# Query and output projections by seven half products each, in a decoder layer on one core

## The chip, the core and the metric

The kernel runs on one core of a Trainium2 chip. The core has an engine for matrix products (PE, whose loads of stationary weights are listed apart as PEld), three engines for other arithmetic (DVE, ACT, POOL) and a queue, SP, that issues all of this kernel's DMAs. [...] PE writes its products into banks of PSUM, DVE and ACT move them from there into SBUF, and POOL works from SBUF to SBUF. The metric is the device time of one execution in microseconds.

## What is computed

The input `x` is four sequences of 2048 positions with 512 features (float32). One pre-norm decoder layer is applied:

```python
x = x + attn(layernorm(x))                # a linear recurrence along the axis of length 4
x = x + xattn(layernorm(x), ctx)          # 16 heads of 32, 77 keys a sequence
x = x + ffn(layernorm(x))                 # 512 -> 2048, butterflies, gelu, butterflies, 2048 -> 512

def xattn(query, context, Wq, Wk, Wv, Wo):
    Q = (query @ Wq.T).reshape(B, T_q, 16, 32)
    K, V = ...                            # from the context, 77 rows
    attn = softmax(Q @ K / sqrt(32))
    return (attn @ V).reshape(B, T_q, 512) @ Wo.T
```

The change concerns `Q` and the product with `Wo`.

## The kernel before

The 2048 positions are cut into 16 blocks `u` of 128. A block holds all four steps `t` of the first axis, so that its `x` is a tile `xt` of 128 positions by 4 steps by 512 features.

Everything that comes ahead of the feed-forward part of a block is the generator `front` (L430). In order: `normed_pairs`, the recurrence as products with fixed taps (`ps_s`, L440), a second norm, the query projection (`ps_q`, L452), the attention steps, the output projection, and a third norm. A norm (`normed`, L402) takes statistics of the four steps on DVE (L377 to L390), then for each step scales on DVE (`xn`, L396), transposes on PE (`ps_t`, L399) and copies on ACT into `xnt` (L400), which holds features on partitions.

- The query projection makes four groups of 128 outputs. Each adds up four products of 512 columns (four steps of 128 positions) in one bank, and ACT copies it to `qt` (L454).
- For each step `t`, four score products go to `ps_sc` (L463), DVE takes maximum and difference (L467, L468), ACT the exponential (L469), DVE sum and reciprocal (L471, L472), and POOL scales the probabilities `pr` (L473). One step later PE transposes them in four groups (`ps_pt`, L483), DVE and ACT copy each group into one of four `pt` tiles, `ps_o` (L494) multiplies them with the values, and DVE copies that to `ot` (L497). Then, for this step alone, four products of 512 columns with `wo` go to `ps_w` (L501), and DVE adds the bank to `xt` (L502).

All banks of `front` carry the tag `f`, of which there are two.

The feed-forward part (`feed_forward`, L522) multiplies by the scheme of Winograd and Strassen: a product of 2x2 halves made by seven products of halves and some sums. The weights are combined before the loop and kept in DRAM (`up7`, `dn7`); `combine` (L510) makes the sums of the block's input, and DVE, ACT and POOL those of the results. All its products have 256 columns (L546, L611). Its weights come by DMA into three rotating buffers (`wts`).

While block `u` is in `feed_forward`, `front` of block `u+1` is woven in: after each pair of products `step` (L531) counts, and at every third count it calls `front` on to its next `yield`. There are 112 counts and 32 yields. A scheduler then sets the order of each engine's instructions. Block 0 has nothing to be woven into but the preparation of the weights (`_prepare`, L213), which runs once at the start; block 15's feed-forward part runs alone at the end.

`wq` and `wo` lie in SBUF through the whole program (L361, L362) and are loaded once (L666, L667).

Of the kernel before, what the change touches and what calls it, by code (L numbers as in the profile page):

```python
# [23 lines left out]
NB = HID // P  # L24
# [188 lines left out]
def _prepare(nc, pool, banks, dram, ident, wexp_t, up_low, up_high, up_bias, dn_low, dn_high, wcon, wup, wdn, bias,  # L213
# [10 lines left out]
    t = wdn  # L224
# [17 lines left out]
    ub = pool.tile([P, NB], F32, name="ub")  # L242
# [4 lines left out]
    nc.sync.dma_start(out=ub, in_=up_bias)  # L247
# [5 lines left out]
    e = _low_products(nc, low, False)  # L253
# [3 lines left out]
    for b in range(NB):  # L257
        ps = banks()
# [33 lines left out]
    nc.vector.tensor_tensor(bias, b1, ub, ALU.add)  # L292
# [16 lines left out]
    src = wcon.rearrange("(p m) d -> p m d", m=NB)  # L309
# [3 lines left out]
    for m in range(NB):  # L313
        ps = banks()
# [5 lines left out]
    src = rows_dn.rearrange("(b p) d -> p b d", p=P)  # L320
# [3 lines left out]
    for b in range(NB):  # L324
        ps = banks()
# [5 lines left out]
    b11, b12, b21, b22 = (wdn[:, r * h : r * h + h, c * (D // 2) : (c + 1) * (D // 2)] for r in range(2) for c in range(2))  # L331
    t1, t2, t3, n4 = (wup[:, i, :].rearrange("p (b d) -> p b d", b=h) for i in range(4))
# [14 lines left out]
def kernel(ctx: ExitStack, tc: tile.TileContext, x, ctx_t, ssm_vec, ssm_vt, ssm_vinv, wq_t, wk_t, wv_t,  # L347
                        wo_t, wexp_t, up_low, up_high, up_bias, dn_low, dn_high, wcon, b_con, down_bias, out):
    nc = tc.nc
    const = ctx.enter_context(tc.tile_pool(name="const", bufs=1))  # L350
    xpool = ctx.enter_context(tc.tile_pool(name="x", bufs=1))
    work = ctx.enter_context(tc.tile_pool(name="work", bufs=2))
    small = ctx.enter_context(tc.tile_pool(name="small", bufs=2))
    dram = ctx.enter_context(tc.tile_pool(name="dram", bufs=1, space=bass.MemoryType.DRAM))
    psum = ctx.enter_context(tc.tile_pool(name="psum", bufs=2, space=bass.MemoryType.PSUM))
# [5 lines left out]
    wq = const.tile([P, NC, D], F32, name="wq")  # L361
    wo = const.tile([P, NC, D], F32, name="wo")  # L362
    hbias = const.tile([P, NB], F32, name="hbias")
    ybias = const.tile([P, D], F32, name="ybias")
    make_identity(nc, ident)
# [61 lines left out]
                yield  # L427
        res.append(xpt)

    def front(u, xt, res):  # L430


        got = []
        yield from normed_pairs(xt, got)
        xpt = got.pop()
        for c in range(NC):
            ps = psum.tile([P, T, P], F32, tag="f", name="ps_s")
            for f in range(P // NS):
                for i in range(T // 2):
                    nc.tensor.matmul(ps[:, 2 * i : T, f * NS : (f + 1) * NS], lhsT=xpt[:, i, c * (P // NS) + f, :],  # L440
                                     rhs=gt[:, 0 : T - 2 * i, :], start=i == 0, stop=i == T // 2 - 1)
            xc = xt[:, :, c * P : (c + 1) * P]
            nc.vector.tensor_tensor(xc, ps, xc, ALU.add)
            yield

        yield from normed(xt, got)
        xnt = got.pop()
        qt = work.tile([P, NC, T, P], F32, tag="qt", bufs=1, name="qt")
        for g in range(NC):
            ps = psum.tile([P, T, P], F32, tag="f", name="ps_q")  # L450
            for c in range(NC):
                nc.tensor.matmul(ps, lhsT=wq[:, c, g * P : (g + 1) * P], rhs=xnt[:, c, :, :],  # L452
                                 start=c == 0, stop=c == NC - 1)
            nc.scalar.copy(qt[:, g, :, :], ps)  # L454
            yield

        probs = [None] * T
        for t in range(T + 1):
            if t < T:
                pr = work.tile([P, NH, NK], F32, tag="pr", name="pr")  # L460
                for g in range(NC):
                    ps = psum.tile([P, 512], F32, tag="f", name="ps_sc")
                    nc.tensor.matmul(ps[:, 0 : 4 * NK], lhsT=qt[:, g, t, :], rhs=kbd[:, t, g, :], start=True, stop=True)  # L463
                    sc = ps[:, 0 : 4 * NK].rearrange("p (j k) -> p j k", j=4)
                    mx = small.tile([P, 4], F32, tag="mx", bufs=4, name="mx")
                    pg = pr[:, 4 * g : 4 * g + 4, :]
                    nc.vector.tensor_reduce(mx, sc, AX.X, ALU.max)  # L467
                    nc.vector.tensor_tensor(pg, sc, mx.unsqueeze(2).to_broadcast([P, 4, NK]), ALU.subtract)  # L468
                    nc.scalar.activation(pg, pg, AF.Exp, scale=1.0 / math.sqrt(DH))  # L469
                sm = small.tile([P, NH], F32, tag="sm", name="sm")  # L470
                nc.vector.tensor_reduce(sm, pr, AX.X, ALU.add)  # L471
                nc.vector.reciprocal(sm, sm)  # L472
                nc.gpsimd.tensor_tensor(pr, pr, sm.unsqueeze(2).to_broadcast([P, NH, NK]), ALU.mult)  # L473
# [5 lines left out]
            pts = []  # L479
            for g in range(NC):  # L480
                pt_ps = psum.tile([P, 4, P], F32, tag="f", name="ps_pt")
                for j in range(4):
                    nc.tensor.transpose(pt_ps[0:NK, j, :], pr[:, 4 * g + j, :], ident)  # L483
                pt = work.tile([NK, 4, P], F32, tag="pt", bufs=4, name="pt")
                if g % 2:
                    nc.scalar.copy(pt, pt_ps[0:NK])
                else:
                    nc.vector.tensor_copy(pt, pt_ps[0:NK])
                pts.append(pt)
            po = psum.tile([P, NC, P], F32, tag="f", name="ps_o")  # L490
            for g in range(NC):
                for j in range(4):
                    h = 4 * g + j
                    nc.tensor.matmul(po[j * DH : (j + 1) * DH, g, :], lhsT=vsb[:, tt, h * DH : (h + 1) * DH],  # L494
                                     rhs=pts[g][:, j, :], start=True, stop=True, tile_position=(0, j * DH))
            ot = work.tile([P, NC, P], F32, tag="ot", bufs=1, name="ot")
            nc.vector.tensor_copy(ot, po)  # L497
            yield
            ps = psum.tile([P, D], F32, tag="f", name="ps_w")
            for g in range(NC):  # L500
                nc.tensor.matmul(ps, lhsT=ot[:, g, :], rhs=wo[:, g, :], start=g == 0, stop=g == NC - 1)  # L501
            nc.vector.tensor_tensor(xt[:, tt, :], ps, xt[:, tt, :], ALU.add)  # L502
            yield
# [18 lines left out]
    def feed_forward(u, xt, rhs, other):  # L522
# [7 lines left out]

        def step():  # L531
            slot[0] += 1
            if slot[0] % 3 == 0:
                next(other, None)

        def bank(tag):
# [115 lines left out]
        return psum.tile([P, 512], F32, tag="abc"[turn[0]], name="ps_p")  # L652

    up7 = [dram.tile([P, 7, 2, P], F32, name=f"up7_{p}") for p in range(NB // 2)]
    dn7 = [dram.tile([P, NB // 2, D // 2], F32, name=f"dn7_{i}") for i in range(7)]
    xts = {0: load_x(0)}
    ready = []
    with tc.tile_pool(name="prep", bufs=1) as pool:
        wup = pool.tile([P, NC, HID], F32, name="wup")
        wdn = pool.tile([P, NB, D], F32, name="wdn")  # L660
        _recurrence_taps(nc, pool, psum, ssm_vec, ssm_vt, ssm_vinv, gt)
        prep = _prepare(nc, pool, banks, dram, ident, wexp_t, up_low, up_high, up_bias, dn_low, dn_high, wcon,
                        wup, wdn, hbias, up7, dn7)
        next(prep)
        _keys_values(nc, psum, ctx_t, wk_t, wv_t, kbd, vsb, wup)
        nc.sync.dma_start(out=wq, in_=wq_t.rearrange("(c p) e -> p c e", p=P))  # L666
        nc.sync.dma_start(out=wo, in_=wo_t.rearrange("(c p) e -> p c e", p=P))  # L667
# [5 lines left out]
        first = front(0, xts.pop(0), ready)  # L673
        for _ in prep:
            next(first, None)
        for _ in first:
            pass
# [80 lines left out]
```

## Time and profile before

| What | Value |
|---|---|
| Median of 3 runs | 2728.86 us (2724.36 to 2729.57) |
| Profiled execution | 2727.85 us, span 2726.1 us |
| First product of a feed-forward part | starts at 237.95 us |
| Period of one block in the loop | 159.0 us |
| PE records of ps_q, of ps_w (128x512) | 512, 512 |
| PE records of L546 and L611 (128x256) | 3584, 3584 |
| DMA | 320.84 MB, mean 118 GB/s |

The profile is one execution taken by the hardware profiler, in microseconds unless ns is written. A line names a source line (L452), an engine, and the tile written. An fp32 product is two MATMUL records. Busy times of PE include the modelled end of its pipeline, so records overlap; starts are better than lengths for a rate. What stands in brackets behind a group, as in `[0.90 <-DVE xn L396]`, is how long the engine was idle ahead of it and what ended that. The chain of waits starts at the last instruction and goes back each time to what released it.

The DMA queue's rows for weights, with engine, count, size of one and median time to landing:

```profile
w_up<-up SPq DMA_DIRECT2D x128, 896.0 KB, 4.6
w_dn<-dn SPq DMA_DIRECT2D x112, 1024.0 KB, 4.8
```

### The profile page before, as it was taken

The page shows a single profiled execution, that of the slowest core. Times are in us where ns is not written, and L with a number is a line of the kernel's source. Part 1 is how long each engine was busy: PE and PEld are TensorE (multiplying, and loading weights), DVE is VectorE, ACT ScalarE, POOL GpSimd, SP SyncE. Part 2 cuts the span into 40 slices and gives each one's busy share as a digit, 9 for nine tenths or more (in the row PEclk, how much of TensorE's full clock was granted, in tenths as well). Part 3 has the DMA queues.
Part 4 walks back from the last instruction along what each step waited for, and adds up shares of the span by engine and source line. Part 5 has one row for each costly group of instructions (what it writes and reads, how often), then busy time and mean ns, then how long its engine had stood idle before and what let it go on. Part 6 is the DMA issues. An engine that isn't in the chain of part 4 may idle for free.

```text
span 2726.1 us, 34675 instructions
## 1 busy us (share of the span) xinstructions
PE 2626.3 (96%) x13448; PEld 2013.5 (74%) x13448; DVE 1308.1 (48%) x3148; ACT 794.3 (29%) x1456; POOL 778.7 (29%) x918
## 2 busy tenths in 40 slices
PE   6887999999999999999999999999999999999999
PEld 4545777786877778687777868777786877778688
DVE  4375544545454454545445454544545454454531
ACT  0222414223241422324142232414223241422321
POOL 4233231413223141322314132231413223141323
PEclk9888999999999999999999999999999999999999
DMA  7664233242423324242332424233232423323244
GB/s 234 213 246 173 89 111 110 78 135 78 143 89 112 111 76 135 78 143 89 113 109 77 135 78 143 89 114 109 76 136 78 143 89 111 112 77 120 78 141 137
DMA packets 96724, 320.84 MB, mean 118 GB/s; under 512 B 17584, under 2 KB 44336, under 8 KB 80432
## 3 DMA queue, kind: packets, MB, share of 16 engines
q1 hardware_dynamic: 96560, 318.62, 34.5%
q8 instruction: 107, 1.75, 0.2%
q14 instruction: 57, 0.47, 0.0%
HBM read 278.47 MB, written 40.12 MB: 117 GB/s over the span
## 4 chain that ended last, share of the span: by engine, by line
PE 83%; DVE 10%; POOL 4%; DMA 1%; issue 1%; ACT 0%; SPq 0%; POOLq 0%; DVEq 0%; ACTq 0%
PE ps_a L611 10%; PE ps_b L546 10%; PE ps_w L501 8%; PE ps_q L452 8%; PE ps_b L611 7%; PE ps_c L546 7%; PE ps_a L546 6%; PE ps_c L611 5%; PE ps_sc L463 5%; PE ps_pt L483 4%; PE ps_s L440 3%; POOL pr L473 2%; PE ps_t L399 2%; PE ps_o L494 2%; DVE st L377 2%
## 5 line engine op out<-in xcount | busy, mean ns | idle before, releaser
L589 POOL TENSOR_TENSOR s<-a,a 128x256 f32<-128x256 f32 x128 | 92.9, 726 | 1120.1 <-ACT a L551 1120.1
L546 PE MATMUL ps_b<-tb,w_up 128*128 128x256 f32 x1536 | 397.0, 379 | 0.7 <-DVE tb L518 0.7
L611 PE MATMUL ps_a<-w_dn,a 128*128 128x256 f32 x1536 | 372.1, 381 | 0.0
L611 PEld LDWEIGHTS ps_a<-w_dn,a 128*128 128x128 f32 x1536 | 282.3, 190 | 57.4 <-issue 20.3
L546 PEld LDWEIGHTS ps_b<-tb,w_up 128*128 128x128 f32 x1536 | 285.9, 190 | 51.1 <-issue 14.5
L551 ACT ACTIVATE a<-a,hbias 128x256 f32<-128x256 f32 x384 | 192.3, 508 | 270.4 <-DVE a L584 206.9
L546 PE MATMUL ps_a<-xnt,w_up 128*128 128x256 f32 x1024 | 269.0, 380 | 0.0
L611 PE MATMUL ps_c<-w_dn,s 128*128 128x256 f32 x1024 | 235.4, 381 | 7.3 <-POOL s L589 7.3
L501 PE MATMUL ps_w<-wo,ot 128*128 128x512 f32 x512 | 236.2, 604 | 4.8 <-DVE ot L497 4.8
L452 PE MATMUL ps_q<-xnt,wq 128*128 128x512 f32 x512 | 231.9, 596 | 0.7 <-ACT xnt L400 0.7
L611 PEld LDWEIGHTS ps_c<-w_dn,s 128*128 128x128 f32 x1024 | 191.0, 190 | 36.8 <-POOL s L589 11.4
L546 PEld LDWEIGHTS ps_a<-xnt,w_up 128*128 128x128 f32 x1024 | 190.4, 191 | 31.2 <-issue 7.2
L473 POOL TENSOR_TENSOR pr<-pr,sm 128x1232 f32<-128x1232 f32 x64 | 146.1, 2282 | 173.1 <-DVE sm L472 162.9
L501 PEld LDWEIGHTS ps_w<-wo,ot 128*128 128x128 f32 x512 | 96.3, 193 | 107.1 <-issue 94.4
L452 PEld LDWEIGHTS ps_q<-xnt,wq 128*128 128x128 f32 x512 | 97.9, 192 | 98.1 <-issue 93.9
L400 ACT COPY xnt<-ps_t 128x512 f32<-128x512 f32 x128 | 72.2, 588 | 331.4 <-PE ps_t L399 331.2
L469 ACT ACTIVATE pr<-pr 128x308 f32<-128x308 f32 x256 | 107.0, 455 | 206.7 <-DVE pr L468 206.2
L463 PE MATMUL ps_sc<-kbd,qt 128*128 128x308 f32 x512 | 163.3, 430 | 3.3 <-DVE pr L468 3.0
L483 PE MATMUL ps_pt<-ident,pr 128*77 128x128 f32 x1024 | 145.4, 281 | 19.2 <-POOL pr L473 13.6
L483 PEld LDWEIGHTS ps_pt<-ident,pr 128*77 128x77 f32 x1024 | 119.3, 150 | 56.5 <-POOL pr L473 19.7
L502 DVE TENSOR_TENSOR xt<-ps_w,xt 128x512 f32<-128x512 f32 x64 | 44.3, 692 | 235.0 <-PE ps_w L501 235.0
L599 POOL TENSOR_TENSOR xt<-xt,ybias 128x256 f32<-128x256 f32 x128 | 100.2, 818 | 184.4 <-DVE xn L396 184.4
(173 smaller groups left out, 3936.4 us busy)
## 6 DMA issues: line engine op xcount, KB each, us to landing
w_up<-up SPq DMA_DIRECT2D x128, 896.0 KB, 4.6
w_dn<-dn SPq DMA_DIRECT2D x112, 1024.0 KB, 4.8
xt<-in_x SPq DMA_DIRECT2D x16, 1024.0 KB, 5.5
out<-xt SPq DMA_DIRECT2D x64, 256.0 KB, 4.9
wdn<-in_wexp_t SPq DMA_DIRECT2D x4, 1024.0 KB, 10.9
rows_up<-wdn SPq DMA_DIRECT2D x16, 256.0 KB, 2.1
wdn<-rows_up SPq DMA_DIRECT2D x4, 1024.0 KB, 9.0
wdn<-in_wcon SPq DMA_DIRECT2D x4, 1024.0 KB, 4.8
```

The lines of the kernel that those rows point to most:

```text
L440: nc.tensor.matmul(ps[:, 2 * i : T, f * NS : (f + 1) * NS], lhsT=xpt[:, i, c * (P // NS) + f, :], rhs=gt[:, 0 : T - 2 * i, :], start=i == ...
L452: nc.tensor.matmul(ps, lhsT=wq[:, c, g * P : (g + 1) * P], rhs=xnt[:, c, :, :], start=c == 0, stop=c == NC - 1)
L463: nc.tensor.matmul(ps[:, 0 : 4 * NK], lhsT=qt[:, g, t, :], rhs=kbd[:, t, g, :], start=True, stop=True)
L469: nc.scalar.activation(pg, pg, AF.Exp, scale=1.0 / math.sqrt(DH))
L473: nc.gpsimd.tensor_tensor(pr, pr, sm.unsqueeze(2).to_broadcast([P, NH, NK]), ALU.mult)
L483: nc.tensor.transpose(pt_ps[0:NK, j, :], pr[:, 4 * g + j, :], ident)
L501: nc.tensor.matmul(ps, lhsT=ot[:, g, :], rhs=wo[:, g, :], start=g == 0, stop=g == NC - 1)
L546: nc.tensor.matmul(ps, lhsT=w[:, c, :], rhs=rhs[i - 1][:, c], start=first and c == 0, stop=c == 1, skip_group_check=True)
L551: nc.scalar.activation(out, x, AF.Gelu, bias=hbias[:, b : b + 1])
L589: nc.gpsimd.tensor_tensor(s1, a21, a22, ALU.add)
L599: nc.gpsimd.tensor_tensor(r, r, ybias[:, d], ALU.add)
L611: nc.tensor.matmul(ps[:, t, :], lhsT=act[p][lhs[i]][:, t, :], rhs=w[:, p, :], start=first and p == 0 and t == 0, stop=p == h - 1, skip_gro ...
```

## The change

Both projections are made by seven products of halves. Weights, input and output are each cut in 2x2 halves. A new generator runs the seven:

```diff
+    def seven(order, lhs, rhs, two, made):
+        tiles = {}
+        for i in order:
+            key = {2: 1, 7: 6, 4: 6, 3: 5}.get(i, i)
+            if key == i:
+                tiles[i] = psum.tile([P, 2, 2 * P], F32, tag="f", name=f"ps_{two}")
+            for r in range(2):
+                for k in range(2):
+                    nc.tensor.matmul(tiles[key][:, r, :], lhsT=lhs(i, r, k), rhs=rhs(i, r, k),
+                                     start=key == i and r == 0 and k == 0, stop=k == 1, skip_group_check=True)
+            made[i](tiles[key])
+            yield
```

Each of the seven is four matmuls of 256 columns, and `made[i]` is its eviction. Products 2, 7, 4 and 3 go on in the bank of an earlier one, after that one has been read. The order is 1, 6, 2, 7, 5, 4, 3.

For the query projection two sums and a difference of the input are made on POOL and DVE, in place where possible, and the results are put together in `qt`:

```diff
-        for g in range(NC):
-            ps = psum.tile([P, T, P], F32, tag="f", name="ps_q")
-            for c in range(NC):
-                nc.tensor.matmul(ps, lhsT=wq[:, c, g * P : (g + 1) * P], rhs=xnt[:, c, :, :],
-                                 start=c == 0, stop=c == NC - 1)
-            nc.scalar.copy(qt[:, g, :, :], ps)
-            yield
+        if wq is None:
+            wq = work.tile([P, 7, NC // 2, D // 2], F32, tag="pt", bufs=1, name="wq")
+            nc.sync.dma_start(out=wq, in_=wq7)
+        nc.gpsimd.tensor_tensor(t3, b22, b12, ALU.subtract)
+        nc.vector.tensor_tensor(b12, b12, b11, ALU.subtract)
+        nc.vector.tensor_tensor(t2, b22, b12, ALU.subtract)
+        right = {1: b11, 2: b21, 3: b22, 4: b21, 5: b12, 6: t2, 7: t3}
+        def second(ps):
+            moved(q11)(ps)
+            nc.gpsimd.tensor_tensor(b21, b21, t2, ALU.subtract)
+        yield from seven((1, 6, 2, 7, 5, 4, 3), ...,
+                         {1: moved(q21), 6: plus(q12, q21), 2: second, 7: plus(q22, q21), 5: plus(q22, q22),
+                          4: plus(q21, q21), 3: plus(q12, q12)})
```

`moved` is an ACT copy of a bank, `plus` a DVE add of a bank and a tile. The seven weights of the query projection no longer stay in SBUF: they are made once (four sums on POOL), stored to DRAM (`wq7`, 1792 KB), and loaded again for each block from 1 on, into the one buffer that the block's `pt` tile takes afterwards. Those of the output projection (`wo`, seven halves) stay in SBUF.

The attention steps keep their work but for the output projection, and `ot` now holds all four steps; `pt` is one tile of four groups with one buffer instead of four tiles. After the last step the output projection runs for all four at once:

```diff
+        nc.gpsimd.tensor_tensor(s1, a21, a22, ALU.add)
+        nc.vector.tensor_tensor(s2, s1, a11, ALU.subtract)
+        nc.gpsimd.tensor_tensor(s3, a11, a21, ALU.subtract)
+        nc.gpsimd.tensor_tensor(s4, a12, s2, ALU.subtract)
+        left = {1: a11, 2: a12, 3: s4, 4: a22, 5: s1, 6: s2, 7: s3}
+        def onto(r):
+            return lambda ps: nc.vector.tensor_tensor(r, ps, r, ALU.add)
+        def spread(ps):
+            nc.scalar.copy(w1, ps)
+            for r in (r12, r22, r21):
+                nc.gpsimd.tensor_tensor(r, r, w1, ALU.add)
+        yield from seven((1, 6, 2, 7, 5, 4, 3), ...,
+                         {1: spread, 6: onto(r12), 2: onto(r11), 7: onto(r22), 5: onto(r22), 4: onto(r21), 3: onto(r12)})
```

`front` has 38 yields now, and `step` spreads them evenly over the first 104 of the 112 counts (`slot[0] * 38 // 104`). The load of `up_bias` goes straight to `hbias`, whose tile saves the small one `ub`.

More of the change, by code (lines that the diff above doesn't have):

```diff
@@ L246, in _prepare @@
     nc.sync.dma_start(out=high, in_=up_high)
-    nc.sync.dma_start(out=ub, in_=up_bias)
+    nc.sync.dma_start(out=bias, in_=up_bias)
     src = wexp_t.rearrange("(b p) d -> p b d", p=P)
@@ L291, in _prepare @@
     nc.sync.dma_start(out=b1, in_=brow[1, :].rearrange("(b p) -> p b", p=P))
-    nc.vector.tensor_tensor(bias, b1, ub, ALU.add)
+    nc.vector.tensor_tensor(bias, b1, bias, ALU.add)
     h, k = HID // 2, NC // 2
@@ L448, in front, with plus, moved @@
         qt = work.tile([P, NC, T, P], F32, tag="qt", bufs=1, name="qt")
-        for g in range(NC):
-            ps = psum.tile([P, T, P], F32, tag="f", name="ps_q")
-            for c in range(NC):
-                nc.tensor.matmul(ps, lhsT=wq[:, c, g * P : (g + 1) * P], rhs=xnt[:, c, :, :],
-                                 start=c == 0, stop=c == NC - 1)
-            nc.scalar.copy(qt[:, g, :, :], ps)
-            yield
+        if wq is None:
+            wq = work.tile([P, 7, NC // 2, D // 2], F32, tag="pt", bufs=1, name="wq")
+            nc.sync.dma_start(out=wq, in_=wq7)
+        b11, b12, b21, b22 = (xnt[:, c : c + 2, t : t + 2, :] for c in (0, 2) for t in (0, 2))
+        q11, q12, q21, q22 = (qt[:, c : c + 2, t : t + 2, :] for c in (0, 2) for t in (0, 2))
+        t3, t2 = (work.tile([P, 2, 2, P], F32, tag="xn", name="tq") for _ in range(2))
+        nc.gpsimd.tensor_tensor(t3, b22, b12, ALU.subtract)
+        nc.vector.tensor_tensor(b12, b12, b11, ALU.subtract)
+        nc.vector.tensor_tensor(t2, b22, b12, ALU.subtract)
+        right = {1: b11, 2: b21, 3: b22, 4: b21, 5: b12, 6: t2, 7: t3}
+        def plus(out, x):
+            return lambda ps: nc.vector.tensor_tensor(out, ps.rearrange("p r (t q) -> p r t q", t=2), x, ALU.add)
+        def moved(out):
+            return lambda ps: nc.scalar.copy(out, ps.rearrange("p r (t q) -> p r t q", t=2))
+        def second(ps):
+            moved(q11)(ps)
+            nc.gpsimd.tensor_tensor(b21, b21, t2, ALU.subtract)
+        yield from seven((1, 6, 2, 7, 5, 4, 3), lambda i, r, k: wq[:, i - 1, k, r * P : (r + 1) * P],
+                         lambda i, r, k: right[i][:, k, :, :], "q",
+                         {1: moved(q21), 6: plus(q12, q21), 2: second, 7: plus(q22, q21), 5: plus(q22, q22),
+                          4: plus(q21, q21), 3: plus(q12, q12)})
         probs = [None] * T
+        ot = work.tile([P, NC, T, P], F32, tag="xnt", bufs=2, name="ot")
         for t in range(T + 1):
@@ L478, in front @@
             pr, tt = probs[t - 1], t - 1
-            pts = []
+            pts = work.tile([P, NC, 4, P], F32, tag="pt", bufs=1, name="pt")
             for g in range(NC):
@@ L494, in front @@
                     nc.tensor.matmul(po[j * DH : (j + 1) * DH, g, :], lhsT=vsb[:, tt, h * DH : (h + 1) * DH],
-                                     rhs=pts[g][:, j, :], start=True, stop=True, tile_position=(0, j * DH))
-            ot = work.tile([P, NC, P], F32, tag="ot", bufs=1, name="ot")
-            nc.vector.tensor_copy(ot, po)
+                                     rhs=pts[0:NK, g, j, :], start=True, stop=True, tile_position=(0, j * DH))
+            nc.vector.tensor_copy(ot[:, :, tt, :], po)
             yield
[L499 to L503, printed above, removed]
+        a11, a12, a21, a22 = (ot[:, g : g + 2, t : t + 2, :] for t in (0, 2) for g in (0, 2))
+        r11, r12, r21, r22 = (xt[:, t : t + 2, d : d + D // 2] for t in (0, 2) for d in (0, D // 2))
+        sw = work.tile([P, 4, 2, 2, P], F32, tag="qt", bufs=1, name="sw")
+        s1, s2, s3, s4 = (sw[:, i] for i in range(4))
+        nc.gpsimd.tensor_tensor(s1, a21, a22, ALU.add)
[3 more added lines that the diff above has]
+        left = {1: a11, 2: a12, 3: s4, 4: a22, 5: s1, 6: s2, 7: s3}
+        w1 = work.tile([P, 2, 2 * P], F32, tag="xn", name="w1")
+        def onto(r):
[4 more added lines that the diff above has]
+                nc.gpsimd.tensor_tensor(r, r, w1, ALU.add)
+        yield from seven((1, 6, 2, 7, 5, 4, 3), lambda i, r, k: left[i][:, k, r, :], lambda i, r, k: wo[:, i - 1, k, :], "w",
+                         {1: spread, 6: onto(r12), 2: onto(r11), 7: onto(r22), 5: onto(r22), 4: onto(r21), 3: onto(r12)})
         yield from normed(xt, got)
@@ L532, in step @@
             slot[0] += 1
-            if slot[0] % 3 == 0:
+            for _ in range(slot[0] * 38 // 104 - (slot[0] - 1) * 38 // 104):
                 next(other, None)
@@ L672 @@
         xts[1] = load_x(1)
-        first = front(0, xts.pop(0), ready)
+        first = front(0, xts.pop(0), ready, wq)
         for _ in prep:
```

28 lines of the change are left out of this document (20 added, 8 removed).

## The prediction

> **What bounds the kernel now.** I read the page's busy shares first, then the busy times of three equal stretches, then the timeline of PE, and last the chain of waits for the rate of each product.
>
> ```profile
> span 2726.1 us, 34675 instructions
> PE 2626.3 (96%) x13448; PEld 2013.5 (74%) x13448; DVE 1308.1 (48%) x3148; ACT 794.3 (29%) x1456; POOL 778.7 (29%) x918
> ...
> 859.00:1018.00 159.00, 156.41 (x818) 121.33 (x817) 77.47 (x188) 48.47 (x89) 44.39 (x50) 1.00 0.32 106
> 1018.00:1177.00 159.00, 156.42 (x818) 121.33 (x817) 77.48 (x188) 48.47 (x89) 44.39 (x50) 1.00 0.31 106
> ```
>
> The columns of the stretches are length, then PE, PEld, DVE, ACT and POOL busy, the granted clock, the DMA share and GB/s. The loop over blocks repeats every 159.0 us, PE is busy for 156.4 of them at clock 1.00, and every other engine has half its time free. So a block is worth what PE issues plus 2.6 us of waits, and the timeline of PE names these:
>
> ```profile
> 913.53 1.08 PE L399 MATMUL ps_t<-ident,xn 128*128 128x128 f32 x8 [0.90 <-DVE xn L396]
> ...
> 956.73 1.10 PE L483 MATMUL ps_pt<-ident,pr 128*77 128x128 f32 x8 [0.91 <-POOL pr L473]
> ...
> 963.51 1.13 PE L611 MATMUL ps_c<-w_dn,s 128*128 128x256 f32 x4 [0.49 <-POOL s L589]
> ...
> 1014.78 1.06 PE L399 MATMUL ps_t<-ident,xn 128*128 128x128 f32 x8 [0.29 <-DVE xn L396]
> ```
>
> The chain of waits gives start, length and what; its lengths run to the next instruction's start, so they are PE's rate, which busy times with their pipelined ends are not:
>
> ```profile
> 920.24 3.43 PE ps_q L452 x8
> ...
> 964.64 3.43 PE ps_w L501 x8
> ...
> 979.81 3.45 PE ps_w L501 x8
> ...
> 1021.90 6.91 PE ps_a L611 x32
> ```
>
> An fp32 product shows as two records. A 128x512 record takes 3.43/8 = 0.429 us (0.431 in the last ps_w), a 128x256 record 6.91/32 = 0.216 us. Half the columns take half the time.
>
> **The change, part by part.** *Products.* Each projection issued 16 products of 512 columns (32 records): 32 x 0.429 = 13.7 us for Q, 32 x 0.431 = 13.8 us for the output. It now issues 7 x 4 = 28 products of 256 columns (56 records), in the form of L546 and L611: 56 x 0.216 = 12.1 us each. Per block: 27.5 - 24.2 = 3.3 us less on PE.
> [...]
>
> *Work beside PE.* Per block DVE gains five Q evictions with an add and two more output adds (7 x 0.69, the L502 row) and three sums of 128x512 (0.68 to 1.61, the L518 and L516 rows below): about 7 to 9 us on 77.5. POOL gains five sums and three adds of `spread` (8 x 1.27, the L630 row): 10 us on 44.4. ACT loses one copy. All have room; only places count.
>
> ```profile
> L516 DVE TENSOR_TENSOR tb<-xnt 128x512 f32<-128x512 f32 x16 | 25.8, 1610 | 0.0
> L518 DVE TENSOR_TENSOR tb<-xnt,tb 128x512 f32<-128x512 f32 x16 | 10.9, 680 | 0.0
> L473 POOL TENSOR_TENSOR pr<-pr,sm 128x1232 f32<-128x1232 f32 x64 | 146.1, 2282 | 173.1 <-DVE sm L472 162.9 <-ACT pt L486 10.1
> L502 DVE TENSOR_TENSOR xt<-ps_w,xt 128x512 f32<-128x512 f32 x64 | 44.3, 692 | 235.0 <-PE ps_w L501 235.0
> ```
>
> *Sums ahead of product 6.* For Q: the last xnt copy (0.6), POOL's t3 (1.3), DVE's b12 and t2 (0.7 each, one DVE add of the FFN 0.4 between, hand-overs 0.2 each) make some 5.2 us, 6.1 with b12 at the 1.61 of L516. On PE stand 6 FFN products (2.6), product 1 (1.7) and 6 more (2.6), 6.9 us. For the output: ot copy, s1 on POOL, s2 on DVE, 3.1 us against 6.0. Cost nothing; without these fillers 3 to 5 us. [...] Products 2, 7, 5, 4 and 3 each stand at least one product and 4 FFN products (3.4 us) behind the eviction they need (0.7 to 2.0): nothing.
>
> *The attention steps lose their cover.* In the changed program's order on PE every inner block is alike. From the first score product to the last `ps_o` stand 16 score products (0.52), 16 groups of transposes (0.435), four `ps_o` (1.01) and only 42 FFN products (0.432): 37.4 us, where the old order also had three ps_w there. Walked by hand with the durations of the timeline (DVE 0.46 and 0.385 a group, sum 1.35, POOL 2.25, hand-overs 0.05 to 0.25): step 0's probabilities come at 13.2 us, PE is there at 11.9 (POOL first serves s1, behind a gelu behind four activation table loads), 1.3 us; steps 1 and 2 are in time; step 3's come at 36.75 against 35.55, 1.2 us; copies of pt cost some 0.6 more. That is 3.1 us, and about 1.0 for changes of product kind, as in the old stretch: there 65.0 us hold 61.6 of products, 3.4 of waits. Taken: +0.7. Bounds: -0.9 (no such wait) and +5.0 (step 0 1.3, step 2 1.5, step 3 the whole 9.2 us that lay between step 0's scores and transposes before, against 6.05 of cover, 3.1; less 0.9).
>
> *The last norm.* Product 3 stands 19 FFN products (8.2 us) ahead of the transposes. On DVE come behind it: its add and two BN statistics 2.2, two FFN adds at L683 and L685 1.2, four BN statistics of the next block interleaved 2.3, small operations 2.6, the first xn 0.7: 9.0. Wait 0.8 instead of 0.3: +0.5, between -0.3 and +2.7. Then the four groups of transposes stand with one product between, and the third and fourth wait for DVE's xn and ACT's copy: +0.6 (0 to 1.2). The middle norm has one product more ahead: -0.2 of its 0.9.
>
> *DMA.* Each block loads wq again, 1792 KB, twice a `w_up` (896 KB, 4.6 us): some 9 us. It is queued on SP behind the fifth w_dn and waits for the last `ps_o`; the sixth w_dn behind it waits for a later product (the end of down 6) anyway and is needed 24 us on, while Q needs wq some 80 us later. Nothing; were it issued late, up to 9 us a block. One pt buffer and a longer `ot` add no wait, since the next step's copies come after the last `ps_o`.
>
> *The front of block 0.* Between 185 and 234 us PE waits on DMA and DVE. Seven output products now come bare at the end, with the next block's four statistics interleaved behind them: 229.1 + 8.4 = 237.5 us instead of 234.2, +3; the start of L326 can slip by some us, as scores now wait behind DVE's s sums. The eight weight sums on POOL (1.3 each) lie in its idle time before 48 us. Taken +4, between -4 and +12. The last FFN is untouched.
>
> *Sum.* 15 x (-3.3 + 0.7 + 0.5 + 0.6 - 0.2) = 15 x -1.7 = -26, +4: -22. The profiled execution took 2727.85 us (span 2726.1), so 2706; the median shown, 2728.86, is 1.0 above it.
>
> **Rivals.**
> *A, the whole gain:* waits stay as they were: 2727.85 - 15 x 3.3 = 2678. For it: periodic, half-idle engines. Against: only 37.4 us are left around the softmax.
> *B, slower:* the softmax chain (DVE, ACT, POOL) becomes PE's bound in the attention steps, where ps_w was its cover. Price: the upper bound, 5.0, and 0.9 of the norms: 15 x (5.9 - 3.3) + 4 = +43, 2771. It decides from 3.3 us of new waits a block. For it: step 0 already waits 0.91 with more cover. Against: DVE has about 29 us of work in the 37.4, and steps 1 and 2 have 10 to 12 us.
> *C, no change:* waits of 2.9 to 3.6 us a block eat it: 2727.85 + 15 x -0.3 + 4 = 2727.
>
> **How the numbers follow.** Forecast (waits of 0.5 to 2.7 a block) 0.58, A 0.10, C 0.11, B and the way to it 0.21. Predicted 2706. The forecast's own range is 2684 to 2722; to leave out no more than 2 in 10 it goes up into C and B, to 2738. Within 0.2% (5.5 us, about what can be told from no change) is C. Faster 0.68, same 0.11, slower 0.21.
>
> **What would show it.** 256-column records of ps_q and ps_w 0.216 us apart; a period near 157.3 us; waits of PE on POOL's pr of about 1.2 us at the first and fourth step, on xn 0.8 at the last norm; no wait of PE on wq. If records of ps_q stand wider than 0.22, the first step is wrong; if pr waits exceed 3 us a block, B holds.

## The result, and the profile after

| | before | after |
|---|---|---|
| Median of 14 runs each | 2728.59 us (2723.71 to 2730.07) | 2732.53 us (2729.52 to 2740.93) |
| Profiled execution, span | 2727.85, 2726.1 us | 2733.22, 2731.4 us |
| First product of a feed-forward part | 237.95 us | 247.38 us |
| Period of one block | 159.0 us | 158.3 us in eight of the thirteen inner ones, 160.0 in five |

The ratio is 1.0021, interval 1.0013 to 1.0029: slower by 0.2%. The forecast was 2706, so the whole gain that was forecast is missing. The page's busy times and two stretches, each one block long (length, then PE, PEld, DVE, ACT and POOL busy, granted clock, DMA share, GB/s):

```profile
PE 2586.7 (95%) x14216; PEld 2163.8 (79%) x14216; DVE 1448.8 (53%) x3308; ACT 748.8 (27%) x1410; POOL 955.1 (35%) x1054
...
407.83:566.12 158.29, 153.39 (x865) 130.39 (x864) 86.36 (x198) 45.40 (x86) 54.75 (x57) 1.00 0.35 118
882.76:1042.74 159.98, 155.08 (x866) 131.56 (x865) 86.37 (x198) 45.42 (x86) 54.78 (x57) 0.99 0.34 117
```

PE has 3.0 us less work a block (156.41 to 153.39), but the block is only 0.7 us shorter: the difference stands idle. In the second stretch the clock is 0.99 and the block 1.7 us longer. The chain of waits shows that the products themselves are as cheap as hoped, 8 records in 1.73 us, 0.216 each:

```profile
922.92 1.73 PE ps_q L439 x8
...
994.60 1.73 PE ps_w L439 x8
```

The timeline of PE names what it waits for:

```profile
964.31 1.10 PE L516 MATMUL ps_pt<-ident,pr 128*77 128x128 f32 x8 [1.84 <-POOL pr L506]
...
988.64 1.10 PE L516 MATMUL ps_pt<-ident,pr 128*77 128x128 f32 x8 [1.00 <-POOL pr L506]
...
1029.77 1.08 PE L397 MATMUL ps_t<-ident,xn 128*128 128x128 f32 x8 [0.20 <-DVE xn L394]
1030.69 0.60 PE L659 MATMUL ps_a<-w_dn,a 128*128 128x256 f32 x2
1033.15 1.17 PE L397 MATMUL ps_t<-ident,xn 128*128 128x128 f32 x8 [1.86 <-DVE w L386]
1034.14 8.76 PE L659 MATMUL ps_c<-w_dn,s 128*128 128x256 f32 x32
```

Before, the waits were 0.90, 0.91, 0.49 and 0.29. The middle norm's 0.90 and the 0.49 on POOL's s are gone; step 0's 0.91 is now 1.84; new are 1.00 at step 3 and 1.86 at the last norm. Look at the last row too: 32 records of FFN (the feed-forward part) that take 7.07 us in most blocks take 8.76 here; the clock granted from 1034.2 to 1037.6 us is 0.50. The same place in the block before:

```profile
875.85 7.07 PE L659 MATMUL ps_c<-w_dn,s 128*128 128x256 f32 x32
```

The longest new wait is put down to `w` of L386, an operation on 4 numbers a partition. DVE's timeline there, and POOL's beside it:

```profile
1027.82 0.12 DVE L386 TENSOR_TENSOR w<-y,v 128x4 f32<-128x4 f32 x1
...
1028.01 0.15 DVE L387 TENSOR_TENSOR w<-w,y 128x4 f32<-128x4 f32 x1
...
1028.21 0.16 DVE L388 SCALAR_TENSOR_TENSOR y<-w,y 128x4 f32<-128x4 f32 x1
...
1029.08 1.00 DVE L394 TENSOR_SCALAR xn<-xt,mv,y 128x512 f32<-128x512 f32 x2
1030.00 0.69 DVE L386 TENSOR_TENSOR w<-y,v 128x4 f32<-128x4 f32 x1
1030.72 0.65 DVE L387 TENSOR_TENSOR w<-w,y 128x4 f32<-128x4 f32 x1
1031.41 0.65 DVE L388 SCALAR_TENSOR_TENSOR y<-w,y 128x4 f32<-128x4 f32 x1
1031.98 1.02 DVE L394 TENSOR_SCALAR xn<-xt,mv,y 128x512 f32<-128x512 f32 x1
```

```profile
1029.70 3.01 POOL L647 TENSOR_TENSOR xt<-xt,ybias 128x256 f32<-128x256 f32 x4 [21.24 <-DVE xn L394]
```

Two scaled steps are made, then three small operations of the *next* block's statistics stand ahead of the third step. They take 0.65 us or more each, where the same lines took 0.12 to 0.16 a few microseconds earlier, while POOL adds `ybias` to the block that has just been normed (four adds, 0.75 each); the third step itself takes 1.02 where each of the first two takes about 0.5. In the kernel before, POOL's adds ran at the same place, but nothing small stood between the steps, and 12 records of FFN stood between PE's groups of transposes:

```profile
1014.09 1.00 DVE L396 TENSOR_SCALAR xn<-xt,mv,y 128x512 f32<-128x512 f32 x2
1015.45 1.42 DVE L396 TENSOR_SCALAR xn<-xt,mv,y 128x512 f32<-128x512 f32 x2 [0.35 <-PE ps_t L399]
```

```profile
1014.71 6.26 POOL L599 TENSOR_TENSOR xt<-xt,ybias 128x256 f32<-128x256 f32 x8 [10.82 <-DVE xn L396]
```

```profile
1015.68 2.76 PE L611 MATMUL ps_b<-w_dn,a 128*128 128x256 f32 x12
```

### The profile page after: what moved, and what is told of

It is laid out like the page before. It is cut to its first block, busy times and chain, and to the rows that moved or that the text cites. A ratio compares the mean times of both kernels' runs of the same rounds, so it can differ in the third digit from the quotient of the medians.

```text
span 2731.4 us, 36576 instructions
## 1 busy us (share of the span) xinstructions
PE 2586.7 (95%) x14216; PEld 2163.8 (79%) x14216; DVE 1448.8 (53%) x3308; ACT 748.8 (27%) x1410; POOL 955.1 (35%) x1054
## 3 DMA queue, kind: packets, MB, share of 16 engines
q8 instruction: 113, 1.85, 0.3%
## 4 chain that ended last, share of the span: by engine, by line
PE 85%; DVE 8%; POOL 5%; DMA 2%; issue 1%; SPq 0%; ACT 0%; DVEq 0%; POOLq 0%; ACTq 0%
PE ps_b L594 12%; PE ps_a L659 9%; PE ps_c L594 8%; PE ps_a L594 8%; PE ps_q L439 7%; PE ps_c L659 7%; PE ps_w L439 7%; PE ps_b L659 7%; PE ps_sc L496 5%; PE ps_pt L516 5%; PE ps_s L454 3%; POOL pr L506 3%; DVE st L375 2%; PE ps_t L397 2%; PE ps_o L526 2%; DVE xn L394 1%
## 5 line engine op out<-in xcount | busy, mean ns | idle before, releaser
L659 PE MATMUL ps_c<-w_dn,s 128*128 128x256 f32 x1024 | 244.4, 389 | 0.0
L659 PEld LDWEIGHTS ps_c<-w_dn,s 128*128 128x128 f32 x1024 | 196.7, 196 | 30.5
L543 DVE TENSOR_TENSOR xt<-ps_w,xt 128x512 f32<-128x512 f32 x96 | 66.4, 691 | 220.0 <-PE ps_w L439 175.9
L439 PE MATMUL ps_q<-xnt,wq 128*128 128x256 f32 x640 | 153.3, 382 | 0.7 <-ACT qt L478 0.7
L676 POOL TENSOR_TENSOR s<-a,s 128x256 f32<-128x256 f32 x128 | 97.5, 775 | 150.3 <-PE ps_b L659 149.4
L669 POOL TENSOR_TENSOR s<-s,a 128x256 f32<-128x256 f32 x128 | 92.2, 726 | 139.8 <-PE ps_c L659 137.7
L500 DVE TENSOR_REDUCE mx<-ps_sc 128x4 f32<-128x308 f32 x256 | 120.3, 475 | 35.5 <-PE ps_sc L496 31.0
```

The source lines that it names most:

```text
L439: nc.tensor.matmul(tiles[key][:, r, :], lhsT=lhs(i, r, k), rhs=rhs(i, r, k), start=key == i and r == 0 and k == 0, stop=k == 1, skip_group ...
L659: nc.tensor.matmul(ps[:, t, :], lhsT=act[p][lhs[i]][:, t, :], rhs=w[:, p, :], start=first and p == 0 and t == 0, stop=p == h - 1, skip_gro ...
L676: nc.gpsimd.tensor_tensor(act[p][4], act[p][1], act[p][4], ALU.subtract)
```

## The experiments

The running theory: the products' gain is real, and waits eat it, at step 0 and step 3 (POOL's probabilities), at the last norm (POOL's adds holding DVE), and through the clock. Periods below are from the first product of one feed-forward part to that of the next.

**1. The adds of ybias spread over the up phase.** Only POOL's order changes.

```diff
+            with tc.issue_after(mark[0]):          # mark: combine's last sum, then each pair's a21
-            nc.gpsimd.tensor_tensor(r, r, ybias[:, d], ALU.add)
+                nc.gpsimd.tensor_tensor(r, r, ybias[:, d], ALU.add)
```

The forecast is for the three small operations of L386 to L388, 0.65 us or more each beside those adds and ahead of the third xn:

> The eight adds of ybias on POOL (L647) are issued one behind each pair's sums through the up phase, instead of all together behind the last norm; the order on PE, DVE and ACT is unchanged. [...] Then they fall to about 0.15, PE's wait of 1.85 us at the last norm falls to 0.2 to 0.4, the period goes from 158.3 to about 156.7, the stretches at half clock (five, each 1.67 us) vanish with the wait, and the time is about 2732 - 14 x 1.6 - 8 = 2702 us. Rival (order on DVE alone: what stands ahead of the third xn is too much whoever else runs): the wait stays at 1.4 us or more, 2728 to 2733. Rival on the clock: if half clock does not come from this wait, some of the five stretches stay: about 2710.

Measured: 2693.76 us, ratio 0.9875 (0.9860 to 0.9889), period 156.31, no half clock behind the front. DVE at the same place in this kernel:

```profile
859.55 1.00 DVE L394 TENSOR_SCALAR xn<-xt,mv,y 128x512 f32<-128x512 f32 x2
860.46 0.16 DVE L386 TENSOR_TENSOR w<-y,v 128x4 f32<-128x4 f32 x1
860.65 0.16 DVE L387 TENSOR_TENSOR w<-w,y 128x4 f32<-128x4 f32 x1
860.85 0.16 DVE L388 SCALAR_TENSOR_TENSOR y<-w,y 128x4 f32<-128x4 f32 x1
860.93 0.54 DVE L394 TENSOR_SCALAR xn<-xt,mv,y 128x512 f32<-128x512 f32 x1
```

```profile
860.24 1.08 PE L397 MATMUL ps_t<-ident,xn 128*128 128x128 f32 x8 [0.21 <-DVE xn L394]
861.16 0.60 PE L664 MATMUL ps_a<-w_dn,a 128*128 128x256 f32 x2
861.62 1.16 PE L397 MATMUL ps_t<-ident,xn 128*128 128x128 f32 x8
```

The same operations in the same order: 0.16 in place of 0.65, and PE's wait of 1.85 is gone. So DVE's order alone did not make the wait; POOL's adds beside it did. The five stretches of half clock went with it, so they came from this wait and not from something apart. The front gained too, which was not in the expectation: the first feed-forward product starts at 242.9 instead of 247.4 us. Of these 4.5 us, 2.8 are there already at the output projection of block 0, before any add of `ybias` runs.

**2. The control: the kernel before with the same spread.** The edit of experiment 1 on the kernel before.

> The kernel before, with ybias spread over the up phase as in the first experiment: the control for it. Theory (POOL's adds cost the kernel before next to nothing, since its last norm had 3.4 us of FFN products between the transposes; the changed order made them cost): period 158.6 to 159.1, time within 6 us of the kernel before, 2720 to 2730. Rival (spreading ybias is a gain for either kernel and says nothing on the change): 2700 us or less.

Measured: 2733.88 us, ratio 1.0016 (1.0007 to 1.0025), period 159.41 instead of 159.0. Spreading the adds costs the old kernel 0.4 us a block, and one new wait stands in a block: 0.25 on xn at the middle norm, where an add of `ybias` now runs beside the scaling (two xn take 1.90 us there, 1.48 before). It is no gain in itself: what it won in experiment 1 is the change's own loss, but for the 2.8 us of the front.

**3. The other side: the next block's statistics behind the last xn.** The adds stay together on POOL, but nothing small stands ahead of the third step on DVE.

```diff
-        mv, y = norm_stats(xt)
+        with tc.issue_after(last_xn[0]) if last_xn[0] else contextlib.nullcontext():
+            mv, y = norm_stats(xt)
```

If it takes the small operations of 0.65 us to make PE's wait of 1.85 us, that wait falls to 0.4 or less and the 0.2 ahead of the first transposes goes too: period 156.3 to 156.6, time 2692 to 2700 us.

> The changed kernel with one order on DVE: the statistics of the next block (L375 to L388) behind the last norm's fourth xn, so that no small operation stands ahead of the third; ybias stays on POOL all at once behind the last norm. [...] Rival (POOL's adds hold the third xn itself as long as they held the small operations): the wait stays above 1 us and the time above 2715. Rival (the statistics are then late for the next block's first transposes): a wait on xp of over 0.5 us takes the place.

Measured: 2694.12 us, ratio 0.9884 (0.9865 to 0.9902), period 156.33, no half clock. From the timelines of PE and of POOL, the one wait left at the last norm, and what POOL does beside it:

```profile
860.49 1.09 PE L400 MATMUL ps_t<-ident,xn 128*128 128x128 f32 x8 [0.38 <-DVE xn L397]
```

```profile
860.42 6.15 POOL L652 TENSOR_TENSOR xt<-xt,ybias 128x256 f32<-128x256 f32 x8 [19.26 <-DVE xn L397]
```

```profile
861.16 1.41 DVE L397 TENSOR_SCALAR xn<-xt,mv,y 128x512 f32<-128x512 f32 x2 [0.36 <-PE ps_t L400]
```

POOL adds as long as before, and the wait is gone all the same, because only xn stood in DVE's way. The edit also moved PE's order a little (four and eight records of FFN between the groups of transposes, in place of two and none), but that is not what took the wait away: the third xn ends at 861.70, and in the old order PE would have come to it at 861.84 (860.49, then eight records of transposes, 0.92, and two of FFN, 0.43). It takes both, the small operations in front and the adds beside them; taking away either gives the same 38 us or so. The 0.2 ahead of the first transposes did not go; it became 0.38.

**4. Step 0's probabilities first on POOL.**

```diff
+            with behind_pr():                      # POOL: behind step 0's scaling
-            nc.gpsimd.tensor_tensor(s1, a21, a22, ALU.add)
+                nc.gpsimd.tensor_tensor(s1, a21, a22, ALU.add)
```

The same stands around `a21` and around the sums of L669.

> On POOL the scaling of step 0's probabilities (L506) is issued ahead of the FFN's sums of the last pair (L637, L638) and of the s1 - a11 sums (L669), which stood ahead of it. Theory (queue order on POOL): sm is ready at 960.3 in the block from 882.8, but POOL serves three FFN sums first and starts at 962.0; put first, the wait of 1.84 us at step 0 falls to 0.5 or less, the period from 158.3 to about 157.0, the time to about 2732 - 14 x 1.3 = 2714 us, with the half clock stretches of the last norm as they were. Rival (the softmax chain on DVE and ACT sets it): the wait stays at 1.4 or more. Rival (the sums put back are missed): what is won at step 0 comes back as a wait of step 1's probabilities or of down 5 or 6 on POOL's sums, 2728 to 2735.

Measured: 2729.85 us, ratio 1.0006 (0.9995 to 1.0016), period 157.94, but seven blocks at 159.6. PE's waits in one block:

```profile
960.73 1.10 PE L519 MATMUL ps_pt<-ident,pr 128*77 128x128 f32 x8 [0.70 <-POOL pr L507]
969.79 0.66 PE L519 MATMUL ps_pt<-ident,pr 128*77 128x128 f32 x4 [0.48 <-POOL pr L507]
986.26 1.10 PE L519 MATMUL ps_pt<-ident,pr 128*77 128x128 f32 x8 [1.07 <-POOL pr L507]
...
1030.78 1.16 PE L398 MATMUL ps_t<-ident,xn 128*128 128x128 f32 x8 [1.85 <-DVE w L387]
```

Step 0's wait fell by 1.1 us, and 0.5 came back at step 1: the second rival in part. POOL's order was a cause of the wait, but POOL has to do the same work in the same short stretch.

**5 and 6. Each projection alone.** For Q alone, the loop over steps has its four `ps_w` products back; for the output alone, Q has its four products of 512 columns. The pace is 35 steps in 104 counts for both.

> Only the query projection by seven half products; the output projection as before, four full products behind each step. Theory (the gain of the products is real, the loss comes from where the output projection stands): 12.1 instead of 13.7 us a block for Q, the attention steps keep their ps_w between scores and transposes, so the waits are near the old ones (0.9 at step 0, 0.3 at the last norm) and no half clock after the front: about 2728 - 15 x 1.6 = 2704 us, period about 157.4. Rival (the sums, the seven evictions or the reload of wq cost what they save): 2725 to 2732, and PE waits on ps_q's operands, on tq or on wq.

> Only the output projection by seven half products, all four steps at once; the query projection by four full products of 512 columns as before (its weights still come anew each block). Theory: the waits of the changed kernel (1.8 and 1.0 at steps 0 and 3, 2 at the last norm) and its half clock stretches and most of the later start of the first FFN (about +9 us) are all here, with only half of the products' gain: about 2732 + 15 x 1.6 = 2756 less what the shorter pace moves, so 2740 to 2760 us. Rival (the loss is shared by both projections): about 2730, and the only-Q kernel near 2730 as well.

Measured: Q alone 2686.29 us, ratio 0.9848 (0.9835 to 0.9861), period 155.42. The output alone 2733.66 us, ratio 1.0022 (1.0012 to 1.0032), period 159.27. All waits of PE in one block, first with Q alone, then with the output alone:

```profile
913.37 1.08 PE L397 MATMUL ps_t<-ident,xn 128*128 128x128 f32 x8 [0.90 <-DVE xn L394]
1019.24 1.06 PE L397 MATMUL ps_t<-ident,xn 128*128 128x128 f32 x8 [0.35 <-DVE xn L394]
```

```profile
917.83 1.08 PE L397 MATMUL ps_t<-ident,xn 128*128 128x128 f32 x8 [0.90 <-DVE xn L394]
961.03 1.10 PE L500 MATMUL ps_pt<-ident,pr 128*77 128x128 f32 x8 [0.91 <-POOL pr L490]
986.37 1.10 PE L500 MATMUL ps_pt<-ident,pr 128*77 128x128 f32 x8 [0.60 <-POOL pr L490]
1028.51 1.09 PE L397 MATMUL ps_t<-ident,xn 128*128 128x128 f32 x8 [0.35 <-DVE xn L394]
1031.21 0.63 PE L397 MATMUL ps_t<-ident,xn 128*128 128x128 f32 x4 [1.18 <-DVE xn L394]
```

Q alone gains 3.6 us a block: 1.6 of products, and the waits of 0.91 and 0.49 on POOL that the kernel before had in its attention steps; counted from start to start of the records, as in the table further down, the gaps in these steps shrink by 1.9, which closes the sum. With the output alone, 1.6 us of products are won and 1.35 more are waited (3.94 against 2.59), all at the steps and the last norm; from start to start the gaps grow by 2.0, which closes this sum too. The expectation for it was too high: its waits are 0.91, 0.60 and 1.18 where the whole change has 1.84, 1.00 and 1.86, and no half clock came.

The two parts do not add up. Alone they gave -1.5% and +0.2%, so -1.3% together, and the whole change gave +0.2%: 1.5%, some 41 us, come from having both. Q adds work for DVE and POOL, and the pace is 38 steps in 104 counts in place of 35, which leaves fewer products between a step's scores and its transposes; which of these does how much was not tried.

**7. Another pace.** With ybias spread as in experiment 1, the block in front advances at uneven steps.

```diff
-            for _ in range(slot[0] * 38 // 104 - (slot[0] - 1) * 38 // 104):
-                next(other, None)
+            while slot[0] >= due[0]:
+                due[0] += next(other, math.inf) or EVEN        # EVEN = 104 / 38
...
-            yield                                              # in seven
+            yield 2.4 if i != 3 or two == "q" else 3.4
...
-                yield                                          # behind a step's scores
+                yield {0: 4.9, 3: 4.2}.get(t)
```

> The kernel with ybias spread over the up phase, and another pace of the block in front beside the FFN: instead of one step every 104/38 = 2.74 FFN products throughout, 4.9 behind step 0's scores and 4.2 behind step 3's, 2.4 behind each half product of the projections. Theory (the attention steps lack FFN products between a step's scores and its transposes, and the half products had more than they need): the waits of 1.85 and 1.0 us on POOL's probabilities fall to 0.3 or less each, none comes in at the projections, the period goes from 156.3 to about 153.8, and the time to about 2694 - 15 x 2.4 = 2658 us. Rival (the softmax chain through DVE, ACT and POOL is served later too, as it stands behind the FFN's own work there, or the projections then wait for their sums): 2680 us or more.

Measured: 2669.89 us, ratio 0.9794 (0.9779 to 0.9810), period 154.83. Step 3's wait is gone, step 0's only fell from 1.85 to 1.51, and no wait came in at the projections:

```profile
946.60 1.10 PE L517 MATMUL ps_pt<-ident,pr 128*77 128x128 f32 x8 [1.51 <-POOL pr L507]
```

Between theory and rival: the cover helped step 3; at step 0 DVE and POOL took other work first (the exponentials end at 939.9 and DVE starts their sum at 941.4; the reciprocal ends at 943.4 and POOL starts the scaling at 944.3).

**8. That work put in order.** To experiment 7 it adds POOL's order of experiment 4, and on DVE the maxima of a step behind the reciprocal of the step before.

```diff
+                    with tc.issue_after(recip) if t else contextlib.nullcontext():
-                    nc.vector.tensor_reduce(mx, sc, AX.X, ALU.max)
+                        nc.vector.tensor_reduce(mx, sc, AX.X, ALU.max)
```

> The kernel with ybias spread and the other pace, and the softmax of a step kept in order on two queues: DVE's maxima and subtractions of a step behind the reciprocal of the step before (they stood ahead of its sum: exp done at 939.9, sum started at 941.4 in the block that waits at 946.6), and POOL's scaling of step 0 ahead of the FFN's sums of the last pair (sm done at 943.4, scaling started at 944.3). Theory (in-order queues of DVE and POOL, not the length of the softmax, make the last wait at step 0): the wait of 1.5 us falls to 0.3 or less, the period from 154.8 to about 153.5, the time from 2670 to about 2650 us. Rival (the FFN's gelus and the exponentials with their table loads on ACT set step 0): the wait stays above 1 us, 2665 us or more. Rival (later scores make steps 1 to 3 wait instead): new waits on POOL's probabilities there that sum to over 1 us, 2663 or more.

Measured: 2647.91 us, ratio 0.9702 (0.9689 to 0.9715), period 153.25. The one wait of PE that is left in a block, and the block's stretch:

```profile
1002.86 1.08 PE L399 MATMUL ps_t<-ident,xn 128*128 128x128 f32 x8 [0.35 <-DVE xn L396]
```

```profile
866.22:1019.47 153.25, 152.85 (x866) 130.44 (x865) 83.82 (x199) 45.68 (x88) 53.97 (x57) 1.00 0.36 122
```

As the theory has it: at this pace the softmax is not too long for its stretch, it was served too late on in-order queues. POOL's order and DVE's were changed together, so their shares are not known. This is the fastest version of all, 3% under the kernel before, but the 3% are not the projections' alone: of the 5.75 us a block, 3.3 are products, and the rest is near what the kernel before waited (2.59, of which 0.35 is left). What its own pace and order could win was not tried.

**9 and 10. The front of block 0 advanced earlier.** 38 (or, with Q alone, 35) steps over the preparation's 26, in place of one for each; the one kernel is otherwise that of experiment 7, the other that with Q alone and ybias spread.

```diff
-        for _ in prep:
-            next(first, None)
+        for k, _ in enumerate(prep):
+            for _ in range((k + 1) * 38 // 26 - k * 38 // 26):
+                next(first, None)
```

> The same, and the front of block 0 advances 38 steps over the 26 of the weight preparation, instead of one step for each and twelve bare ones at the end. Theory (the first FFN starts late because twelve steps, the output projection and the last norm among them, stand bare at the end of the preparation): the first FFN product at about 235 instead of 243 us, the time about 8 us under the kernel with the pace alone, some 2650. Rival (the preparation is bound by its transfers and DVE's work, and the front only moves about in it): within 2 us of the kernel with the pace alone.

> Only the query projection by seven, with ybias spread and the front of block 0 advanced 35 steps over the 26 of the preparation. Theory: the period stays at 155.3 to 155.4 (its waits are 0.9 and 0.3 on xn, not on POOL), the first FFN starts near 242 instead of 252.1 us, so about 2676 us. Rival (the preparation is bound by transfers and DVE): 2684 to 2688. If the kernel with pace and preparation is under this one, the output projection by seven is worth having once its waits are gone.

Measured: with the pace of experiment 7, 2672.03 us (0.9807, 0.9789 to 0.9824), the first feed-forward product at 245.8 against 245.5 us: no difference from experiment 7, so the rival holds. With Q alone and ybias spread, 2680.97 us (0.9836, 0.9821 to 0.9851): the first feed-forward product comes at 249.2 us (expected near 242, without the edit 252.1) and the second block's feed-forward part starts at 398.0 instead of 410.1, but the period is 155.82 instead of 155.42, the same 0.4 us that the spread cost the kernel before. So the steps advanced earlier won some 12 us at the front with Q alone and nothing with the pace of experiment 7; why, these runs do not show.

## Why the prediction was wrong

By its own terms, in us a block. The measured column adds up the distances from one PE record's start to the next, less the rate of its kind, place by place, in one block at full clock of each kernel:

| Step of the prediction | Predicted | Measured |
|---|---|---|
| Products | -3.3 | -3.3 |
| Attention steps | +0.7 | +1.5 (step 0 +0.9, step 3 +1.2, wait on POOL's s and the ps_o groups -0.6) |
| Middle norm | -0.2 | -1.0 |
| Last norm, with its transposes close together | +1.1 | +2.0 |
| Remainder | | +0.1 |
| Period | -1.7 | -0.7 |
| Half clock (five blocks at 1.67, over fifteen) | 0 | +0.6 |
| Front of block 0, once | +4 | +9.4 |

Fifteen periods at -0.71 are -10.6; half clock adds 8.4, the first and last block, whose neighbours differ, -2.0, the front 9.4 and the tail 0.2: +5.4 us, as the profiled executions differ (2733.22 - 2727.85). The forecast was -22, so 27 us are missing: the last norm and the half clock that follows from it make 22 of them, the front 5. The attention steps' 0.8 too little and the middle norm's 0.8 too much cancel, which is luck.

*Products:* right, in the rate (0.216 us), in the sums beside them (DVE +8.9, POOL +10.4 a block against 7 to 9 and 10), in the sums ahead of product 6 and in the reload of wq, at none of which PE waits.

*Attention steps:* the mechanism was named and its places too, step 0 and step 3; sizes were 1.3 and 1.2 and are 1.84 and 1.00. Step 0 was too low because three of the FFN's sums stood ahead of the scaling on POOL, where the walk by hand had one; with the sums behind it the wait fell by 1.1 (experiment 4).

*The middle norm:* predicted -0.2, for one product more ahead of it; the whole wait went. DVE at its first xn, before and after:

```profile
911.65 0.67 DVE L390 SCALAR_TENSOR_TENSOR y<-w,y 128x4 f32<-128x4 f32 x1
912.36 1.48 DVE L396 TENSOR_SCALAR xn<-xt,mv,y 128x512 f32<-128x512 f32 x2
```

```profile
916.59 0.16 DVE L388 SCALAR_TENSOR_TENSOR y<-w,y 128x4 f32<-128x4 f32 x1
916.78 1.00 DVE L394 TENSOR_SCALAR xn<-xt,mv,y 128x512 f32<-128x512 f32 x2
```

In the kernel before, POOL made two sums of FFN beside them (911.6 to 913.1); in the changed kernel the norm comes some 3 us after such a pair. These rows take 1.0 us less: the hold that the change made at the last norm stood here before it. This is read from the traces; no run tried it apart.

*The last norm:* here the prediction failed. It priced "the four groups of transposes stand with one product between" at 0.6 (0 to 1.2) from hand-overs of xn and the copy, and the chain of DVE by the durations of its rows. The chain came out shorter than taken (0.2 of wait ahead of the first transposes; predicted 0.8). The third group waited 1.85 us: three small operations of the next block stand between the second and the third xn, where the prediction, which put 2.6 us of small operations ahead of the first, names none, and beside POOL's adds each takes 0.65 us, not 0.15. POOL's `ybias` adds follow at once on each xn, since they wait for the old `xt` to be read, and hold DVE. In the kernel before they ran at the same place, but no small operation stood there and 12 records of FFN stood between the transposes; the change took both away. So the +0.6 for the four groups is the term that was too small, and the hold of DVE by POOL is what it left out: the last norm cost +2.0, and +0.6 of half clock with it. The prediction had the two rows of 1610 and 680 ns for one DVE form before it and used them for Q's sums only. The traces show 0.65 us for these small operations beside adds of 0.75 and 0.16 without them (experiment 1); what makes POOL hold DVE was not shown.

*Half clock:* no step of the prediction held it. It is a consequence of the last norm's wait, shown by experiments 1 and 3, and cost 8.4 us in this execution.

*The front:* +9.4 lies within the bounds given. It can be read in three pieces:

```profile
232.41 1.89 PE L439 MATMUL ps_w<-wo,sw 128*128 128x256 f32 x8
242.08 1.94 PE L397 MATMUL ps_t<-ident,xn 128*128 128x128 f32 x8 [7.79 <-DVE xn L394]
245.64 1.94 PE L397 MATMUL ps_t<-ident,xn 128*128 128x128 f32 x8 [1.62 <-DVE xn L394]
```

The last output product ends at 234.1 instead of 229.1, where the prediction had left it: 5.1. From there to the transposes it is 7.9 us instead of 5.1: 2.8, near the 3 predicted for the next block's statistics; with these statistics behind the last xn (experiment 3) it is 5.9. The rest, 1.5, is the hold of DVE by POOL's adds again (the wait of 1.62), gone in experiments 1 and 3. The 5.1 are not explained: the output projection of block 0 ends 2.8 us earlier in experiment 1 and 0.7 in experiment 3, though neither edit is aimed at what stands ahead of it.

*The rivals:* the time is nearest to the rival of no change, which asked for waits of 2.9 to 3.6 us a block; the waits are 2.6, and 3.2 with the half clock's 0.6. It named no place or mechanism beyond that sum, so that it came nearest is luck. The slower rival had the right place, the attention steps without `ps_w` as cover, but the steps alone cost 1.5, not 5.0.

## What to carry to other kernels

Where a change takes filler products from between two dependent groups on PE, or lets another block's small operations in between, look at everything that runs on DVE and POOL *at that moment*, the next block's small operations and the last block's leftovers included: here operations of 0.15 us took 0.65 while POOL added beside them. Price each engine's queue by what is issued ahead of the operation that PE needs, not by how busy the engine is: DVE and POOL were idle for 45% and 65% of the block, and the pace and the order of their queues decided 46 us (2694 to 2648). Try the parts of a change apart, and don't expect them to add up: here one of two halves gained 1.5% and the other lost 0.2%, the whole lost 0.2%, and moving eight adds turned that into a gain of 1.2%.

## What the runs showed of the hardware

In five of the changed kernel's fourteen blocks with a wait of 1.85 us at the last norm, the clock granted to PE fell to 0.50 after it. The clock records of its trace lie on a grid of 3.41 us that does not move with the blocks (158.3 us are 46.4 steps of it): the five half stretches behind the front start at 1034.2, 1194.6, 1512.0, 1672.5 and 2307.3 us, whole multiples of 3.413 apart, and each lasts one step of it. Laid against that grid, the last norm's waits that began 0.10 to 0.97 us into a step were followed by a step at half clock in 12 of 12 blocks (5 here, 7 in experiment 4), those that began elsewhere (at 0.07 or less, or at 1.31 or more) in 0 of 16. The bounds are drawn from these 28 blocks and were not tried on others. Each costs 1.67 us, about half a step: the 32 records of 8.76 us above. The longest run of this kernel, 2740.93 us, also has its lowest mean clock, 0.984 against 0.986 to 0.988 in the others, but the clock doesn't explain every difference among them. The equal wait of 1.84 us at step 0 was followed by half clock in none of 45 blocks (this kernel, experiments 1 and 3), though 12 of these waits began in the same part of a step; what differs there (transposes of 77 columns instead of 128, what stands around them) was not tried.
